# Two of batch 1's token tiles, instead of one, through all eight experts of layer 1

## The chip, the cores and the metric

The kernel runs on one core of a Trainium2 chip. The core has five engines with one instruction queue each, and each queue runs in order: TensorE (PE: matmuls and transposes, PEld its weight loads), VectorE (DVE), ScalarE (ACT), GpSimd (POOL) and SyncE (SP, which here only issues DMAs). The metric is the device time of one execution in microseconds (us). Before the change three runs gave 1483.84, 1483.90 and 1484.85 us; their median is 1483.9.

## The reference

The input x has 2 batches of 1024 tokens of 128 numbers, all in f32. Two layers follow, each an attention and a mixture of experts, with a layernorm ahead of each part and a residual sum behind it. The change lies in layer 1's mixture of experts:

```python
logits = relu(xf @ Wr1 + br1) @ Wr2 + br2
tg, ti = top_k(softmax(logits), 2)
tg = softmax(tg / 2)
out = silu(xf @ Ws1 + bs1) @ Ws2 + bs2            # shared expert, every token
for e in range(8):
    h = silu(xf @ We1[e] + be1[e]) @ We2[e] + be2[e]
    out = out + sum(tg * (ti == e)) * h           # two of eight experts a token
```

Each token needs two of the eight experts. The result is the same whether a token goes through its two experts alone, or through all eight with a weight of zero for six of them.

## The kernel before

A batch is 8 token tiles of 128. The instructions of PE, DVE, ACT and POOL stand in the order in which the Python code emits them (`manual_schedule`); those of SP are ordered by the framework's own planner. The parts of layer 1's experts are Python generators: each `next` emits one step, and the code around them decides whose step comes next.

- **Attention of layer 1** is a loop over `i` from 0 to 130. Unit `i` is (batch, query tile `qt`, head pair `pr`), with 8 units to a query tile, so batch 1 has the units 64 to 127 and iterations 128 to 130 drain the pipeline. One iteration issues the scores of unit `i` (L1082, PE), the maxima (L1090, DVE) and exponentials (L1112, ACT), the transposes of unit `i-1` (L1124, PE), their copies out of PSUM (L1130, ACT and DVE), and the product with the values of unit `i-2` (L1163, PE). The row of `qt` = 6 is batch 1's seventh, i = 112 to 119; that of `qt` = 7 is i = 120 to 127.
- **`route1(b, t0, nt)`** is the router of `nt` tiles, 9 steps (10 for one tile): statistics (L833), a root on POOL (L108), the normalised `y` on ACT (L840), transposes (L846) and an SP write of `y` to DRAM when `nt` > 1 (L849), a bias sum on POOL (L851), the two router matmuls (L856, L861), and the choice of two experts with some 20 small DVE operations and two of ACT (`picks`, L176 to L209).
- **`send1(b, nt)`** sorts the tokens of the first `nt` tiles by expert, one after another mostly on DVE: `places` (L280 to L321) and `tokens_of` (L335 to L375, with `2*nt` matmuls at L357). It takes 12 steps for 7 tiles, 11 for 6 (one 512-wide DVE step fewer). Sorted tokens are put into tiles of one expert each: `sorted_tiles(8)` = 23, `sorted_tiles(7)` = 21, `sorted_tiles(6)` = 19.
- **`experts1`** goes through the sorted tiles, one a step: a gather from DRAM on POOL (L911), a 256 KB weight load on SP (L898, four buffers `we1`), up-matmuls (L950), bias (L884, DVE), tanh (L887, ACT), L892 (DVE), down-matmuls (L958), a transpose of a later tile (L963), L966 (DVE), L941 (ACT) and a scatter to DRAM on POOL (L942). **`combine1`** reads the scattered rows back (L1017), adds them and stores the output (L1024, L1006).
- **`all_experts1(b, t)`** takes one tile in its own order through all eight experts, without sort, gather or scatter: L991, L884, L887, L892, L998, L1001, L984 and a sum on POOL (L985); 11 steps.
- **`shared1(b, n)`** is the shared expert of four tiles (L1044, L1055), 8 steps.

In the loop, `work(i)` emits one step of the list `side`, whose elements run one after another: `route1` and `send1` of batch 0, two `shared1`, `route1(1, 0, 4)`, and then, no earlier than i = `last` = 123, `route1(1, 4, 3)` and `send1(1, 7)`. It is called once an iteration from i = 67 on, and twice from `last` on. Every second iteration from 96 on emits one step of batch 0's `experts1`. What is left after the loop forms the tail:

- the rest of `side`, each step beside one of `route1(1, 7, 1)` and every second one beside a step of batch 0's experts;
- batch 0's remaining experts beside the first gathers of batch 1's (`after`), then `after` with 21 sorted tiles, beside both `shared1` of batch 1;
- tile 7 through `all_experts1`, beside `combine1` of tiles 0 to 6, and the last store.

Of the kernel before, what the change touches and what calls it, by code (L numbers as in the profile page):

```python
# [11 lines left out]
F32 = mybir.dt.float32  # L12
# [7 lines left out]
P = 128  # L20
# [3 lines left out]
NT = T // P  # L24
QB = 512
NQB = T // QB
TPB = QB // P
# [4 lines left out]
NE = 8  # L32
# [19 lines left out]
def two_layers(ctx, tc, a, out):  # L52
# [334 lines left out]
    with ExitStack() as st:  # L387
# [103 lines left out]
        N = len(units)  # L491
# [376 lines left out]
    def send1(b, nt):  # L868

        got = []  # L870
        yield from places(hots[b][:, :, :nt], got)
        rows, tiles_of[b] = got
        yield
        got = []
        yield from tokens_of(rows, gains[b][:, :, :nt], got)
        rows_of[b] = got
        yield
# [93 lines left out]

    def all_experts1(b, t):

        gate = small.tile([P, 2, NE], F32, tag="gate1", name="gate1", bufs=1)
        for k in range(2):
            nc.vector.tensor_tensor(gate[:, k, :], hots[b][:, k, t, :], bc(gains[b][:, k, t:t + 1], [P, NE]), ALU.mult)
        nc.vector.tensor_tensor(gate[:, 0, :], gate[:, 0, :], gate[:, 1, :], ALU.add)
        h, o = {}, {}
        up = {e: expert_weights(e) for e in range(UP_AHEAD)}
        for i in range(NE + 3):  # L980
            if i + UP_AHEAD < NE:
                up[i + UP_AHEAD] = expert_weights(i + UP_AHEAD)
            if i >= 3:
                nc.scalar.mul(o[i - 3], o[i - 3], gate[:, 0, i - 3:i - 2])  # L984
                nc.gpsimd.tensor_tensor(xs[b][:, t, :], xs[b][:, t, :], o.pop(i - 3), ALU.add)  # L985
            if 1 <= i <= NE:
                h[i - 1] = hidden1(*h[i - 1])
            if i < NE:
                ps = bank()
                for f in range(NI):  # L990
                    nc.tensor.matmul(ps[:, f * P:(f + 1) * P], up[i][:, f * P:(f + 1) * P], norms[b][:, t * P:(t + 1) * P],  # L991
                                     start=True, stop=True)
                h[i] = biased1(ps, be1[:, i * NI:(i + 1) * NI])
            if 2 <= i <= NE + 1:
                e = i - 2
                ps = bank()
                for f in range(NI):
                    nc.tensor.matmul(ps[:, :C], h[e][:, f * P:(f + 1) * P], we2[:, (e * NI + f) * C:(e * NI + f + 1) * C],  # L998
                                     start=(f == 0), stop=(f == NI - 1))
                o[e] = f1.tile([P, C], F32, tag="o1", name="o1", bufs=6)  # L1000
                nc.vector.scalar_tensor_tensor(o[e], ps[:, :C], 0.5, be2[:, e * C:(e + 1) * C], ALU.mult, ALU.add)  # L1001
            yield
# [5 lines left out]
    def combine1(b, nt, wait):  # L1008

        for _ in range(wait):  # L1010
            yield
        z = a1.tile([P, 2, NT, C], F32, tag="pT", name="z", bufs=2)
        groups = [(t0, min(TPB, nt - t0)) for t0 in range(0, nt, TPB)]
        for t0, n in groups:
            for k in range(2):
                rows = k * T + t0 * P
                nc.sync.dma_start(out=z[:, k, t0:t0 + n], in_=results[b][rows:rows + n * P, :].rearrange("(t p) c -> p t c", p=P))  # L1017
        for _ in range(4):
            yield
        for t0, n in groups:  # L1020
            yield
            xv = xs[b][:, t0:t0 + n, :]
            for k in range(2):
                nc.vector.tensor_tensor(xv, z[:, k, t0:t0 + n], xv, ALU.add)  # L1024
            store(b, t0, n)
# [34 lines left out]
    with ExitStack():  # L1060
        units = [(b, qt, pr) for b in range(NB) for qt in range(NT) for pr in range(8)]
        N = len(units)
# [121 lines left out]
        with tc.manual_schedule(engines={ET.PE, ET.DVE, ET.Activation, ET.Pool}):  # L1184
            steps = prepare(1)
            experts = experts1(0, NT, AHEAD)


            last = N // 2 + 8 * (NT - 1) + 3
            side = [(N // 2 + 3, route1(0, 0, TPB, "ckv", "lnT")), (0, route1(0, TPB, TPB, "ckv", "lnT")),  # L1190
                    (0, send1(0, NT)), (0, shared1(0, 0)), (0, shared1(0, 1)),
                    (N // 2 + 8 * TPB + 3, route1(1, 0, TPB, "k0", "k1")),
                    (last, route1(1, TPB, 3, "k0", "k1")), (0, send1(1, NT - 1))]

            def work(i):

                while side and i >= side[0][0] and next(side[0][1], N) is not None:
                    side.pop(0)

            issued = {}  # L1200

            def issue(i):
                s = scores(i)
                issued[i] = maxima(i, s)

            for i in range(N + 3):
                ends = units[i - 1][:2] if 1 <= i <= N and units[i - 1][2] == 7 else None
                ahead = short(i) and short(i + 1)
                if i < N and i not in issued:
                    if ahead:  # L1210
                        issue(i)
                    else:
                        s = scores(i)
                if ahead:

                    issue(i + 1)
                if 1 <= i <= N:
                    probsT[i - 1] = a1.tile([P, 2 * NT, P], F32, tag="pT", name="pT", bufs=2)
                    ps = fill(i - 1, 0)
                    if not short(i - 1):  # L1220
                        for r in range(2):
                            evict(i - 1, 0, r, ps, nc.scalar.copy)
                if i < N:
                    if i in issued:
                        exponentials(i, *issued.pop(i))
                    else:
                        exponentials(i, *maxima(i, s))
                if 1 <= i <= N and short(i - 1):
                    evict(i - 1, 0, 0, ps, nc.vector.tensor_copy)
                    evict(i - 1, 0, 1, ps, nc.scalar.copy)  # L1230
                if ends:
                    recips[ends] = reciprocals(ends)
                if i >= last:
                    work(i)
                if 2 <= i <= N + 1:
                    values(i - 2)
                    if units[i - 2] == (0, NT - 1, 7):
                        spread_values(1)
                if 1 <= i <= N and not short(i - 1):
                    ps = fill(i - 1, 1)  # L1240
                    for r in range(2):
                        evict(i - 1, 1, r, ps, nc.vector.tensor_copy)
                probs.pop(i - 1, None)
                if i >= 3 and units[i - 3][2] == 7:
                    project_out(*units[i - 3][:2])
                work(i)
                if i >= N // 2 + 8 * TPB and i % 2:
                    next(experts, None)
                if i < N:
                    b, qt, pr = units[i]  # L1250

                    if b == 0 and qt >= 2 and (i % 2 or qt >= NT - 2) and (left > 6 or (qt, pr) >= (NT - 2, 3)):
                        next(steps, None)
                        left -= 1
                    if (b, qt, pr) == (0, NT - 1, 4):
                        for _ in steps:
                            pass
                    if qt + 1 < NT and pr == 0:
                        mask_queries(b, qt + 1)
                    elif b + 1 < NB and (qt, pr) == (NT - 1, 5):  # L1260
                        mask_queries(b + 1, 0)

            def run(*steps):

                return any([next(g, N) is None for g in steps])


            half, rest = shared1(1, 0), chain(route1(1, NT - 1, 1, "k0", "k1"), shared1(1, 1))
            k = 0
            while side:  # L1270
                work(N)
                if k % 2 == 0:
                    run(experts)
                run(rest)
                k += 1
            after = experts1(1, NT - 1, 1)
            for k in range(AHEAD):
                run(after)
                run(half) if k % 2 else run(experts)
            while run(experts):  # L1280
                run(after)
            combining = combine1(0, NT, 6)
            while run(after):
                run(half) or run(rest)
                run(combining)
            while run(half) or run(rest):
                pass
            dense, combining = all_experts1(1, NT - 1), combine1(1, NT - 1, 0)
            while run(combining, dense):
                pass  # L1290
            store(1, NT - 1, 1)


# [67 lines left out]
```

## Time and profile before

| of the profiled execution | |
|---|---|
| its device time | 1485.42 us |
| its span, first to last instruction | 1483.6 us |
| mean granted TensorE clock | 0.977 |
| PE busy / PEld / DVE / ACT / POOL | 92% / 67% / 70% / 61% / 18% |
| chain that ended last, by engine | PE 70%, DVE 16%, ACT 6%, issue 5% |

The span is the time between the first and the last instruction in the trace. Busy is the time in which an engine ran at least one instruction. A row of the timeline gives start, duration, engine, line, operation, names and shape, the number of instructions merged into it, and in brackets the idle time of the engine before it and what ended it. A row of the windows view gives a stretch, its length, the busy time of PE, PEld, DVE, ACT and POOL with the instructions of each, the granted TensorE clock (1.00 is full), and the load of the DMA engines.

### The profile page before, as it was taken

Reading aid. Unit: us, or ns where it says so; the run is one execution under the profiler, and the core shown is the slowest. Engines: PE = TensorE matmul, PEld = TensorE weight load, DVE = VectorE, ACT = ScalarE, POOL = GpSimd, SP = SyncE. Lnnn points to the kernel's source line nnn. Section 1 sums busy time; section 2 is a strip of 40 time slices with the busy share of each in tenths; the row PEclk is TensorE's granted clock in tenths of the full one; section 3 lists DMA queues with packets and bytes.
Section 4 is the critical chain, followed back from the end, with each engine's and each line's share of the span. In section 5 each row is a group of like instructions: output and inputs, shape, how many; then the busy total and the mean of one; then the engine's idle time right before and its main releaser. Section 6 shows DMA issues by size and latency. Waiting matters only on the chain.

```text
span 1483.6 us, 40458 instructions
## 1 busy us (share of the span) xinstructions
PE 1369.4 (92%) x16931; PEld 986.8 (67%) x16931; DVE 1033.1 (70%) x2344; ACT 904.1 (61%) x1913; POOL 269.4 (18%) x246
## 2 busy tenths in 40 slices
PE   5999999999999999999998979999987899988787
PEld 3776777777777767777765555666754577757676
DVE  3776667777756867777457568677879467877476
ACT  4777567767755776776432257876665577753343
POOL 1010010000000100000154551012021212214553
PEclk9999999999999999999999989999989999999899
DMA  4000000000000000000110030000000011112443
GB/s 110 2 16 16 16 2 16 16 16 17 16 16 2 16 16 16 17 16 3 30 35 1 1 91 2 2 2 2 2 16 30 15 30 34 50 30 72 129 131 110
DMA packets 31318, 43.14 MB, mean 29 GB/s; under 512 B 7545, under 2 KB 19506, under 8 KB 31138
## 3 DMA queue, kind: packets, MB, share of 16 engines
q1 hardware_dynamic: 25216, 28.47, 6.9%
q0 software_dynamic: 4352, 10.70, 2.8%
q8 instruction: 134, 2.20, 0.6%
q10 hardware_dynamic: 1570, 1.41, 0.4%
q14 instruction: 46, 0.38, 0.1%
HBM read 35.51 MB, written 5.05 MB: 27 GB/s over the span
## 4 chain that ended last, share of the span: by engine, by line
PE 70%; DVE 16%; ACT 6%; issue 5%; another core or an unknown queue 1%; DMA 1%; POOL 0%; DVEq 0%; SPq 0%; ACTq 0%; POOLq 0%
PE ps_s L501 15%; PE ps_a L568 12%; PE ps_t L551 8%; PE ps_s L1082 8%; PE ps_t L1124 4%; PE ps_s L253 3%; PE ps_a L1163 3%; DVE ps_s L1090 3%; DVE p L510 3%; PE ps_a L486 2%; PE ps_t L950 2%; PE ps_t L958 2%; PE ps_t L583 2%; ACT p L1112 2%; DVE p L1090 2%
## 5 line engine op out<-in xcount | busy, mean ns | idle before, releaser
L510 DVE CUSTOM_DVE_ANT_0 p<-ps_s,zero 128x1024 f32<-128x1024 f32 x256 | 303.4, 1222 | 135.6 <-PE ps_s L501 134.3
L520 ACT ACTIVATE p<-p,nmx 128x1024 f32<-128x1024 f32 x256 | 293.1, 1153 | 3.1 <-DVE nmx L510 3.0
L557 ACT COPY pT<-ps_t 128x512 f32<-128x512 f32 x256 | 137.5, 589 | 197.7 <-PE ps_t L551 197.7
L501 PE MATMUL ps_s<-qk 64*128 64x512 f32 x1024 | 253.2, 609 | 1.9 <-DVE nmx L510 1.4
L568 PE MATMUL ps_a<-pT,zv 128*64 128x128 f32 x4096 | 251.8, 276 | 0.0
L568 PEld LDWEIGHTS ps_a<-pT,zv 128*64 128x64 f32 x4096 | 220.9, 137 | 9.3 <-issue 0.8
L551 PEld LDWEIGHTS ps_t<-ident,p 64*128 64x128 f32 x4096 | 159.9, 139 | 90.2 <-issue 86.5
L557 DVE COPY pT<-ps_t 128x512 f32<-128x512 f32 x256 | 164.6, 685 | 54.1 <-PE ps_t L551 54.1
L1082 PE MATMUL ps_s<-k,qm 64*128 64x512 f32 (+3 forms) x768 | 172.0, 536 | 16.6 <-ACT p L1112 11.7
L551 PE MATMUL ps_t<-ident,p 64*128 64x64 f32 x4096 | 177.5, 226 | 1.3 <-DVE pT L557 0.7
L1090 DVE CUSTOM_DVE_ANT_0 p<-ps_s,cmask 128x640 f32<-128x640 f32 (+3 forms) x128 | 126.0, 1022 | 71.8 <-PE ps_s L1082 60.7
L542 POOL TENSOR_TENSOR aoT<-aoT,recip 128x1024 f32<-128x1024 f32 x16 | 37.9, 2371 | 660.3 <-DMA recip<-flat 432.9
L501 PEld LDWEIGHTS ps_s<-qk 64*128 64x128 f32 x1024 | 92.9, 189 | 84.4 <-issue 74.5
L1124 PEld LDWEIGHTS ps_t<-ident,p 64*128 64x128 f32 x2304 | 106.4, 141 | 53.1 <-issue 25.5
L1130 ACT COPY pT<-ps_t 128x512 f32<-128x512 f32 (+3 forms) x192 | 95.8, 533 | 74.2 <-PE ps_t L1124 70.4
L1112 ACT ACTIVATE p<-p,nmx 128x640 f32<-128x640 f32 (+3 forms) x128 | 125.9, 992 | 4.6 <-DVE nmx L1090 4.5
L1082 PEld LDWEIGHTS ps_s<-k,qm 64*128 64x128 f32 x768 | 74.0, 196 | 82.1 <-issue 43.7
L1124 PE MATMUL ps_t<-ident,p 64*128 64x64 f32 x2304 | 119.3, 229 | 7.6 <-DVE pT L1130 2.9
L1163 PE MATMUL ps_a<-pT,vx 128*32 128x128 f32 x2304 | 99.1, 281 | 9.0 <-DVE pT L1130 8.3
L1130 DVE COPY pT<-ps_t 128x128 f32<-128x128 f32 (+3 forms) x192 | 87.2, 482 | 8.4 <-remote 5.9
L887 ACT ACTIVATE th<-h 128x512 f32<-128x512 f32 x52 | 32.8, 630 | 88.2 <-DVE h L884 78.4
L1112 ACT ACTIVATE p<-ps_s,nmx 128x128 f32<-128x128 f32 (+3 forms) x128 | 66.3, 525 | 31.3 <-DVE nmx L1090 30.6
(252 smaller groups left out, 1807.2 us busy)
## 6 DMA issues: line engine op xcount, KB each, us to landing
we<-in_we SPq DMA_DIRECT2D x52, 256.0 KB
recip<-flat SPq DMA_DIRECT2D x32, 256.0 KB
we<-in_we POOLq DMA_DIRECT2D x1, 2048.0 KB
z<-results SPq DMA_DIRECT2D x6, 256.0 KB
x<-in_x SPq DMA_DIRECT2D x4, 256.0 KB
up<-in_up_proj POOLq DMA_DIRECT2D x1, 1024.0 KB
normed<-y SPq DMA_DIRECT2D x3, 256.0 KB
out_x<-x SPq DMA_DIRECT2D x3, 256.0 KB
```

The costliest lines, as they stand in the source:

```text
L501: nc.tensor.matmul(s[h][:, n * QB:(n + 1) * QB], qk[rows, 0, qt * P:(qt + 1) * P], qk[rows, 1, n * QB:(n + 1) * QB], start=True, stop=True)
L510: nc.vector.tensor_tensor_reduce(p, s, bc(zero, [P, T]), -1.0, 3e38, ALU.add, ALU.min, nmx)
L520: nc.scalar.activation(p, p, AF.Exp, bias=nmx, scale=-1.0, accum_out=ssum[:, h, qt:qt + 1])
L551: nc.tensor.transpose(ps[r][:, k * 64:(k + 1) * 64], probs[i][h][rows, k * P:(k + 1) * P], ident[rows, rows])
L557: copy(probsT[i][h][:, :, r * 64:(r + 1) * 64], ps[r].rearrange("p (j q) -> p j q", q=64))
L568: nc.tensor.matmul(acc[h * D0:(h + 1) * D0, cols], zv[:, j, :], probsT[i][h][:, j, :], start=(j == 0), stop=(j == NT - 1))
L1082: nc.tensor.matmul(s[h][:, n * QB:n * QB + w], qms[b, qt][rows, pr, :], kTs[b][pr // 4][rows, n * QB:n * QB + w], start=True, stop=True)
L1090: nc.vector.tensor_tensor_reduce(to[:, :nk], s[:, :nk], cmask[:, T - nk:], -1.0, 3e38, ALU.add, ALU.min, nmx)
L1112: nc.scalar.activation(p[:, h, :nk], s[h][:, :nk], AF.Exp, bias=nmx[h], scale=-1.0, accum_out=sums[b, qt][:, head:head + 1])
L1124: nc.tensor.transpose(ps[r][:, c * 64:(c + 1) * 64], probs[i][rows, h, j * P:(j + 1) * P], ident[rows, rows])
L1130: copy(probsT[i][:, 8 * f:8 * f + n, r * 64:(r + 1) * 64], ps[r][:, :n * 64].rearrange("p (j q) -> p j q", q=64))
L1163: nc.tensor.matmul(acc[to * 32:(to + 1) * 32, k * P:(k + 1) * P], vx[:, j, g, pr % 4 * 24:pr % 4 * 24 + 32], probsT[i][:, h * (qt + 1) + j ...
```

## The change

The number of sorted tiles of batch 1 becomes `ND` = 6, and the tiles 6 and 7 go through `all_experts1`. `last` becomes 64 + 8*6 + 3 = 115, so the router of tiles 4 and 5 and the sort of six tiles may be emitted 8 iterations earlier, and `work` is called twice an iteration from 115 on. The router of tiles 6 and 7 (`prep`, 9 steps) stands after the loop, beside the first gathers and batch 0's experts. The second dense tile begins 8 steps after the first, and each has its own store. The small `gate1` tile gets a second buffer.

```diff
-        gate = small.tile([P, 2, NE], F32, tag="gate1", name="gate1", bufs=1)
+        gate = small.tile([P, 2, NE], F32, tag="gate1", name="gate1", bufs=2)
...
-            last = N // 2 + 8 * (NT - 1) + 3
+            ND = NT - 2
+            last = N // 2 + 8 * ND + 3
...
-                    (last, route1(1, TPB, 3, "k0", "k1")), (0, send1(1, NT - 1))]
+                    (last, route1(1, TPB, ND - TPB, "k0", "k1")), (0, send1(1, ND))]
...
-            half, rest = shared1(1, 0), chain(route1(1, NT - 1, 1, "k0", "k1"), shared1(1, 1))
-            k = 0
+            prep, half = route1(1, ND, NT - ND, "k0", "k1"), chain(shared1(1, 0), shared1(1, 1))
             while side:
                 work(N)
-                if k % 2 == 0:
-                    run(experts)
-                run(rest)
-                k += 1
-            after = experts1(1, NT - 1, 1)
+                run(experts)
+                run(prep)
+            after = experts1(1, ND, 1)
             for k in range(AHEAD):
                 run(after)
+                run(prep)
                 run(half) if k % 2 else run(experts)
+            while run(prep):
+                run(experts) or run(half)
             while run(experts):
                 run(after)
             combining = combine1(0, NT, 6)
             while run(after):
-                run(half) or run(rest)
+                run(half)
                 run(combining)
-            while run(half) or run(rest):
+            while run(half):
                 pass
-            dense, combining = all_experts1(1, NT - 1), combine1(1, NT - 1, 0)
-            while run(combining, dense):
+            def dense(t):
+                yield from all_experts1(1, t)
+                store(1, t, 1)
+            combining = chain(combine1(1, ND, 0))
+            first, second = dense(ND), dense(ND + 1)
+            for _ in range(NE):
+                run(combining, first)
+            while run(combining, first, second):
                 pass
-            store(1, NT - 1, 1)
```

## The prediction, made before the changed kernel ran

> **What bounds it now.** I read the page first, then the TensorE timeline of batch 1's last two attention rows, then the windows view of the stretch behind them, then the chain.
>
> ```profile
> span 1483.6 us, 40458 instructions
> PE 1369.4 (92%) x16931; PEld 986.8 (67%) x16931; DVE 1033.1 (70%) x2344; ACT 904.1 (61%) x1913; POOL 269.4 (18%) x246
> ```
>
> TensorE is the bound. The timeline shows how far this holds beside a side step. First the seventh row with one side step an iteration, then the eighth with two:
>
> ```profile
> 1255.20 1.77 PE L1082 MATMUL ps_s<-k,qm 64*128 64x512 f32 x8
> ...
> 1258.92 1.16 PE L950 MATMUL ps_t<-xT,we 128*128 128x128 f32 x8
> ...
> 1261.01 1.77 PE L1082 MATMUL ps_s<-k,qm 64*128 64x512 f32 x8
> ...
> 1264.73 0.66 PE L846 MATMUL ps_t<-ident,y 128*128 128x128 f32 x4
> 1265.32 1.77 PE L1082 MATMUL ps_s<-k,qm 64*128 64x512 f32 x8
> ...
> 1313.26 1.20 PE L846 MATMUL ps_t<-ident,y 128*128 128x128 f32 x3 [2.43 <-ACT y L840]
> 1314.39 3.53 PE L1082 MATMUL ps_s<-k,qm 64*128 64x512 f32 x8
> ...
> 1337.93 2.02 PE L958 MATMUL ps_t<-we,h 128*128 x8 [3.22 <-DVE pT L1130]
> ```
>
> With one step the matmuls follow without a gap: a unit costs 3.72 (1255.20 to 1258.92), an expert step 2.09 (to 1261.01), the router's transposes 0.59. With two, TensorE waits 2.43 for `y` and 3.22 for copies that stand on DVE behind `picks`, and the scores after the first gap take 3.53 instead of 1.77 to 1.99. The windows of the eighth row (two rows, drain included) and the tail:
>
> ```profile
> 1298.80:1328.50 29.70, 24.97 (x335) 16.97 (x334) 19.88 (x47) 16.64 (x35) 7.21 (x7) 0.94 0.16 37
> 1328.50:1349.30 20.80, 15.69 (x216) 12.38 (x212) 16.47 (x60) 8.23 (x19) 3.92 (x4) 0.92 0.14 31
> 1349.30:1364.70 15.40, 12.36 (x88) 11.26 (x88) 12.31 (x39) 5.29 (x16) 5.13 (x6) 0.89 0.24 77
> 1364.70:1389.50 24.80, 20.42 (x142) 19.04 (x142) 13.59 (x26) 10.38 (x25) 15.59 (x15) 0.86 0.42 113
> 1389.50:1457.00 67.50, 55.14 (x409) 48.94 (x408) 42.30 (x96) 29.21 (x72) 33.44 (x33) 0.95 0.49 135
> 1457.00:1483.60 26.60, 17.48 (x136) 15.85 (x136) 15.20 (x33) 8.40 (x18) 7.65 (x11) 0.96 0.34 102
> ```
>
> The tail is 134.3 us: A, the rest of the sort (15.4); B, sorted experts and shared expert (24.8 + 67.5 = 92.3); C, the dense tile (26.6). In B the chain holds two stops that no instruction explains:
>
> ```profile
> 1372.01 4.11 another core or an unknown queue
> ...
> 1392.97 6.79 another core or an unknown queue
> ```
>
> **Step count.** Sorted tiles go from 21 to 19, dense steps from 8 to 16: six expert steps more, all of them work for TensorE. They must be paid for by A and by waits.
>
> **C.** Steady dense steps:
>
> ```profile
> 1463.93 1.16 PE L998 MATMUL ps_t<-we,h 128*128 128x128 f32 x8 [0.54 <-DVE h L884]
> 1464.93 1.06 PE L991 MATMUL ps_t<-lnT,we 128*128 128x128 f32 x8
> 1465.98 1.16 PE L998 MATMUL ps_t<-we,h 128*128 128x128 f32 x8
> ```
>
> They repeat every 2.05 us. The second tile starts 8 steps after the first and overlaps its last three, so C gains 8 x 2.05 = +16.5. Its eight weight loads are on SP three to four steps (6 to 8 us) ahead; the first tile's store stands between them on SP and waits for its last sum on POOL, about one step, which that lead covers; uncovered it would cost 2. The read-back of results (L1017, issued 1462.36 in the profile) stays at the start of C. The second `gate1` buffer only lets the second tile's three small DVE operations go ahead: 0.
>
> **B.** Before, B holds 9 - 3 = 6 steps of batch 0 and 21 of batch 1. The two shared experts take about 14.2 there (for each four L1044 groups of 0.86 and two L1055 groups of 1.8). So an expert step costs (92.3 - 14.2) / 27 = 2.89, stops and half clock included. After: A's three steps join, 9 + 19 = 28 steps, 80.9, plus 14.2. The router for two tiles brings nine steps where B had four. Its root on POOL now queues behind gathers and scatters (0.98 + 0.30 each), and DVE, in order, waits for it with the experts' bias sums behind; it also writes 128 KB of `y` on SP that nobody reads, ahead of weight loads with three steps' lead. I take 3 for the five extra steps (0 if the experts cover them, 6 if each delays a step by a DMA issue). B becomes 98.1. A and B together go from 107.7 to 98.1, -9.6; the tail by -9.6 + 16.5 = +6.9.
>
> **Attention.** `side` needs 75 steps after; 48 are called before i = 115, the rest at two an iteration, so it ends at i = 128: no sort is left for the tail and A goes. The price is 14 iterations at double rate (115 to 128) where there were 8 (123 to 130), of which 13 instead of 5 lie in full attention. The five cost: i = 123 to 126 took 29.7 us; their own TensorE work is 4 x 4.05 (eighth-row unit, 1298.79 to 1302.84) + 2 x 2.09 + 1.9 for the router = 22.3; i = 127 took 11.6 (1328.46 to 1340.10) against 6.15. Together 12.9 us of loss, 2.6 an iteration. The single-rate row above lost nothing. For after I take: i = 115 to 118, `route1(1, 0, 4)` with `y` and its transposes in one iteration as in the row of 2.43: 4 x 2.6 = 10; i = 118 to 122, the router of two tiles, with `y` and transposes in different iterations: half, 6; the sort, i = 123 to 128: DVE needs 4.5 an iteration for attention and experts plus 9.7 / 5.5 for the sort (11.0 us for seven tiles), 6.3 against some 5.5 on TensorE: 7. Sum 23, so +10. Between what ends lie these? Below, 0 (all like the single-rate row); above, 13 x 2.6 = 34. Further, L357 and the sort's other matmuls move into full rows, +2.5; the drain loses DVE's sort operations ahead of the last output (1345.07 to 1348.18), -3. Attention: +9.5.
>
> **Two rules weighed.** After the 2.43 gap and inside the 3.22 one the granted clock fell to half: 1.5 lost in the scores and 1.4 at 1337.93 and behind. The Trainium skill (TensorE: Matmul & The Clock Gate, "Why this matters for your kernels") asks for no idle gap over about 3 us between matmuls. Read so, most of the new gaps (1 to 2.6 us) would keep the clock, and the 23 fall to about 18: 5 us less. I keep the row. Against my forecast speaks the skill's Perfetto Trace Analysis, "Optimization Strategy": regimes with different bounds may gain by interleaving. By it A's work other than its experts vanishes beside attention, attention costs 0, and the sum is +7. The row without gaps says that attention has no free TensorE time, only that a single step costs nothing beyond its own work.
>
> **Sum.** +9.5 + 6.9 = +16.4, rounded down to +15 because the sort's and router's costs are taken from the worst iterations. The profiled span, 1483.6, is 0.3 below the median of the runs, 1483.9; the profiled device time, 1485.4, is 1.5 above. I add to the median: **1499 us**; likeliest case alone 1492 to 1507.
>
> **Rivals.**
> - *Attention hides it* (the interleaving rule): double rate costs nothing more than before. 1483.9 + 6.9 = 1491. For it: the seventh row, where the router now runs, has a little less DVE work (maxima of 1.0 to 1.1 us instead of 1.1 to 1.2). Against: the waits for `y` are of order, not of load.
> - *Faster, by the loss of the last five iterations going away.* If the 12.9 belongs to the eighth row's full DVE and not to the double rate, it vanishes with the router moved up. Then attention is -12.9 + 2.5 - 3 plus what the new 14 iterations lose. At nothing lost: 1483.9 - 13.4 + 6.9 = 1477. It decides where they lose under 3.6 us together. Against: the sort still sits in the eighth row, with more DVE work than the router's.
> - *The stops go away.* The stops of 4.1 and 6.8 fall where POOL issues gathers back to back, and half clock follows (6.8 us lost in B). With gathers spread over other steps they may not come: -17.7 on the sum, about 1482, no change. Nothing names their cause, so I can't say that they go.
> - *Worse:* all 13 iterations lose 2.6: +11 more, 1510; the same if the dense pair waits for weights.
> - *It doesn't do what it says:* a sort still open at the loop's end. The count excludes it.
>
> **Chances.** Main case 0.48, hidden in attention 0.17, faster 0.15, stops gone 0.08 (a quarter of it below 0.2%, the rest within), worse 0.12. Measurement tells 0.2%, 3 us, from no change. Faster 0.17, same 0.06, slower 0.77. The range leaves out most of the faster case and the end of the worse one: 1481 to 1510.
>
> **What would show it.** Right: 16 L991 groups instead of 8 at about 2.05, C near 43 us; no L357 behind the last L1163; gaps over 1 us ahead of L846 or L958 from i = 115 on; last scores some 10 us later than 1328.46. Wrong: last scores not later than before; expert steps in B under 2.5 us; a gap ahead of L991 released by a DMA.

## The result and the profile after

The changed kernel takes **1505.4 us** in the median of four runs (1502.98 to 1510.41), the kernel before 1484.4 in four runs beside it: a ratio of **1.0134 [1.0113, 1.0155]**, slower by 21 us. The forecast was 1499, with a range of 1481 to 1510. The execution that was profiled took 1502.98 us, the lowest of the four, and that of before 1485.42, 1.0 above its median, so the traces show 17.5 us of the difference (span 1501.1 against 1483.6) and not the whole 21.

The first lines of the page of after: the span, then busy time, share and instructions of each engine.

```profile
span 1501.1 us, 40680 instructions
PE 1382.3 (92%) x17021; PEld 997.3 (66%) x17021; DVE 1042.3 (69%) x2363; ACT 910.3 (61%) x1923; POOL 270.4 (18%) x250
```

TensorE is busy 12.9 us longer than before, part of it at half clock; the other 4.6 us of the longer span are waits.

I cut both traces at four marks that exist in both: the scores of unit 114, the scores of unit 123, the last projection of the attention (L1179), and the first matmul of a dense tile (L991). The windows view of before:

```profile
1250.36:1298.79 48.43, 48.00 (x684) 35.58 (x683) 42.01 (x106) 35.21 (x76) 11.54 (x11) 1.00 0.15 47
1298.79:1349.19 50.40, 40.56 (x544) 29.24 (x544) 36.26 (x106) 24.88 (x53) 11.13 (x11) 0.93 0.16 34
1349.19:1457.99 108.80, 88.99 (x642) 80.34 (x643) 68.40 (x160) 45.27 (x114) 54.88 (x54) 0.92 0.44 121
1457.99:1483.60 25.61, 16.52 (x130) 14.86 (x128) 15.12 (x32) 8.00 (x17) 6.93 (x10) 0.96 0.36 106
```

and of after:

```profile
1253.10:1315.82 62.72, 54.07 (x692) 39.28 (x691) 46.55 (x131) 36.69 (x80) 13.30 (x14) 0.95 0.14 39
1315.82:1361.65 45.83, 39.88 (x559) 30.27 (x559) 36.25 (x94) 23.65 (x50) 7.83 (x8) 0.96 0.14 31
1361.65:1458.72 97.07, 79.89 (x584) 71.24 (x583) 60.97 (x138) 43.25 (x107) 52.74 (x50) 0.95 0.45 129
1458.72:1501.10 42.38, 32.66 (x258) 29.68 (x256) 27.24 (x59) 15.38 (x33) 11.57 (x18) 0.95 0.37 111
```

| stage | before | after | difference | forecast |
|---|---|---|---|---|
| units 114 to 123 | 48.4 | 62.7 | +14.3 | |
| unit 123 to last projection | 50.4 | 45.8 | -4.6 | attention in all +9.5 |
| sorted tail (A and B) | 108.8 | 97.1 | -11.7 | -9.6 |
| dense tail (C) | 25.6 | 42.4 | +16.8 | +16.5 |

The last 2.7 us lie ahead of unit 114; 2.0 of them in the first 42 us of the kernel, where the change touches nothing. The first line of each fence is the finding: in the seventh row TensorE went from 48.00 busy of 48.43 at full clock to 54.07 of 62.72 at 0.95. It has only 8 matmuls more there: of the 14.3 us, 8.2 are waits and 6.1 are busy time, most of it matmuls at a lower clock.

The TensorE timeline of after shows the waits that were named:

```profile
1263.79 1.56 PE L846 MATMUL ps_t<-ident,y 128*128 128x128 f32 x4 [2.07 <-ACT y L840]
1265.14 1.94 PE L950 MATMUL ps_t<-xT,we 128*128 128x128 f32 x8
...
1281.33 1.16 PE L958 MATMUL ps_t<-we,h 128*128 x8 [1.34 <-DVE pT L1130]
...
1301.31 0.62 PE L856 MATMUL ps_t<-lnT,wr 128*32 128x256 f32 x2 [2.28 <-ACT lnT L847]
1301.86 3.08 PE L1082 MATMUL ps_s<-k,qm 64*128 64x512 f32 x8
...
1343.25 2.15 PE L1082 MATMUL ps_s<-k,qm 64*128 64x512 f32 x7
```

`y` of the first four tiles comes 2.07 late, and its transposes then take 1.56 where they took 0.66 before; the expert step (L950), which doesn't use `y`, stands behind them in the queue and waits too; the router matmul of tiles 4 and 5 waits 2.28 for the transposed tile, and the scores behind it take 3.08. The last scores stand at 1343.25, 14.8 later than at 1328.46.

The dense tail, TensorE and then SP's queue:

```profile
1484.80 1.16 PE L998 MATMUL ps_t<-we,h 128*128 128x128 f32 x8
1485.80 1.06 PE L991 MATMUL ps_t<-lnT,we 128*128 128x128 f32 x8
1486.85 1.16 PE L998 MATMUL ps_t<-we,h 128*128 128x128 f32 x8
```

```profile
1482.43 0.34 SPq L1006 DMA_DIRECT2D out_x<-x  x1
1482.88 0.37 SPq L898 DMA_DIRECT2D we<-in_we  x1
```

The dense steps repeat every 2.05 us as before. The first tile's store does stand between the weight loads on SP, and no L991 group waits for a DMA behind it.

### The profile page after: what moved, and what is told of

It reads as the page before. It is cut to its first block, busy times and chain, and to the rows that moved or that the text cites. A ratio compares the mean times of both kernels' runs of the same rounds, so it can differ in the third digit from the quotient of the medians.

```text
span 1501.1 us, 40680 instructions
## 1 busy us (share of the span) xinstructions
PE 1382.3 (92%) x17021; PEld 997.3 (66%) x17021; DVE 1042.3 (69%) x2363; ACT 910.3 (61%) x1923; POOL 270.4 (18%) x250
## 4 chain that ended last, share of the span: by engine, by line
PE 69%; DVE 17%; ACT 6%; issue 5%; another core or an unknown queue 1%; DMA 1%; POOL 0%; ACTq 0%; SPq 0%; DVEq 0%; POOLq 0%
PE ps_s L501 15%; PE ps_a L568 12%; PE ps_t L551 8%; PE ps_s L1082 7%; PE ps_t L1124 3%; PE ps_s L253 3%; PE ps_a L1163 3%; DVE ps_s L1090 3%; DVE p L510 2%; PE ps_a L486 2%; PE ps_t L958 2%; PE ps_t L583 2%; PE ps_t L950 2%; ACT p L1112 2%; PE ps_t L718 1%
## 5 line engine op out<-in xcount | busy, mean ns | idle before, releaser
L1082 PE MATMUL ps_s<-k,qm 64*128 64x512 f32 (+3 forms) x768 | 172.8, 538 | 16.7 <-ACT p L1112 11.8
L1163 PE MATMUL ps_a<-pT,vx 128*32 128x128 f32 x2304 | 99.0, 280 | 9.1 <-DVE pT L1130 8.5
L887 ACT ACTIVATE th<-h 128x512 f32<-128x512 f32 x58 | 36.6, 630 | 91.3 <-DVE h L884 72.4
```

Of the source, the lines that this page charges most:

```text
L1082: nc.tensor.matmul(s[h][:, n * QB:n * QB + w], qms[b, qt][rows, pr, :], kTs[b][pr // 4][rows, n * QB:n * QB + w], start=True, stop=True)
L1163: nc.tensor.matmul(acc[to * 32:(to + 1) * 32, k * P:(k + 1) * P], vx[:, j, g, pr % 4 * 24:pr % 4 * 24 + 32], probsT[i][:, h * (qt + 1) + j ...
```

## The experiments

The kernels ran on several chips, and these differ: the kernel before takes 1484 us on the first one, 1459, 1456 and 1486 on three others. So each run is read by its ratio to the kernel before on its own chip, and by its stages. Some expectations give absolute times made for the first chip; on a faster chip these don't apply and their ratios do. All stages in one table (us):

| kernel | 114 to 123 | 123 to projection | sorted tail | dense tail | ratio to before |
|---|---|---|---|---|---|
| before, first chip | 48.4 | 50.4 | 108.8 | 25.6 | |
| after, first chip | 62.7 | 45.8 | 97.1 | 42.4 | 1.0134 [1.0113, 1.0155] |
| before_again | 48.4 | 48.1 | 88.6 | 25.7 | one execution |
| after_again | 61.8 | 46.3 | 83.2 | 42.4 | 1.0098 [1.0060, 1.0137] |
| e1_double123 | 48.4 | 42.7 | 91.4 | 42.1 | 1.0048 [1.0030, 1.0067] |
| e2_single | 48.4 | 37.7 | 98.0 | 42.0 | 1.0093 [1.0071, 1.0116] |
| e3_one_dense | 61.8 | 44.8 | 81.5 | 25.0 | 1.0007 [0.9989, 1.0025] |
| e4_plain_gather | 61.6 | 44.8 | 79.4 | 44.2 | 1.0113 [1.0092, 1.0133] |
| s7_shared_late | 46.0 | 49.4 | 104.1 | 25.6 | 1.0025 [1.0011, 1.0038] |
| s6_shared_late | 47.2 | 46.1 | 95.6 | 42.1 | 1.0086 [1.0059, 1.0112] |
| e5_parity | 58.9 | 52.1 | 97.1 | 42.1 | 1.0110 [1.0090, 1.0130] |
| e6_prep_spread | 62.7 | 45.7 | 94.2 | 42.4 | 1.0098 [1.0074, 1.0121] |
| b1_double127 | 48.5 | 39.6 | 114.0 | 25.6 | 0.9966 [0.9955, 0.9976] |

e1 to e4 ran on the chip of 1459, the two repeats, s7 and s6 on that of 1456, e5, e6 and b1 on that of 1486.

### Two steps an iteration only from i = 123, as before

Six sorted and two dense tiles stay, and so do the units at which router and sort may start; only the second step an iteration comes later. The router of tiles 6 and 7 moves behind what is left of the sort.

```diff
-                if i >= last:
+                if i >= N // 2 + 8 * (NT - 1) + 3:
                     work(i)
...
             while side:
                 work(N)
                 run(experts)
-                run(prep)
```

> Edit: the changed kernel, but two side steps an iteration only from i = 123 on; the router of tiles 4 and 5 may still start at 115. The end of the sort (3 or 4 steps) falls behind the loop, beside batch 0's experts. Theory (the double rate costs): iterations 114 to 122 fall from 62.7 us to about 48 as before the change, 123 to the last projection rises from 45.8 to about 50, sorted tail 97 to about 101: -6, 1497 to 1501 us. Rival (a side step costs the same at any rate, only the six added expert steps cost): attention stays near 108 us, the tail grows by the left sort, 1507 to 1511.

Units 114 to 123 went back to 48.4, from 61.8 in e3, which has after's attention and ran on the same chip. The stretch behind, now with sort steps at double rate, took 42.7, less than expected. The tail pays for the sort steps left over: 91.4 against 81.5. The windows view of e1, first three stages:

```profile
1245.82:1294.23 48.41, 47.99 (x684) 35.60 (x683) 42.00 (x106) 35.11 (x76) 11.52 (x11) 1.00 0.15 47
1294.23:1336.89 42.66, 37.47 (x541) 27.80 (x541) 35.94 (x106) 24.17 (x52) 10.76 (x11) 0.96 0.17 38
1336.89:1428.30 91.41, 81.75 (x609) 72.66 (x608) 64.09 (x151) 43.52 (x109) 51.98 (x50) 0.96 0.45 137
```

The same router of tiles 0 to 3 runs beside the same attention units here, TensorE is busy 47.99 of 48.41, and the clock is full. So neither the router nor the seventh row costs the 13 us, but the second step in an iteration. From unit 114 to the projection it is 91.1 against 106.7 in e3, 15.6 less, and the tail gives 9.9 of that back. The ratio is 1.0048, against 1.0098 in after_again on another chip; the two intervals still overlap, so the reading rests on the stages of one chip.

### One step an iteration to the end

```diff
-                if i >= last:
-                    work(i)
...
-                run(prep)
```

> Edit: the changed kernel with one side step an iteration throughout; the whole sort of six tiles stands behind the loop, each step beside a step of batch 0's experts. Theory (the double rate costs): from unit 114 to the last projection 84 to 88 us instead of 108.5, no idle gap of TensorE over 1 us ahead of a router matmul; sorted tail up from 97 to about 112; total 1492 to 1503. Rival (steps cost the same at any rate): 11 fewer steps of about 1 us there, attention 97 to 100, and a total of 1508 or more.

Attention has no loss left: from unit 114 to the last projection 86.1 us (48.4 and 37.7). TensorE's timeline of e2 at the places where after waits for `y` and for the transposed tile:

```profile
1259.66 0.66 PE L846 MATMUL ps_t<-ident,y 128*128 128x128 f32 x4
...
1263.96 1.05 PE L856 MATMUL ps_t<-lnT,wr 128*32 128x512 f32 x2
...
1308.61 0.44 PE L846 MATMUL ps_t<-ident,y 128*128 128x128 f32 x2
...
1316.24 0.62 PE L856 MATMUL ps_t<-lnT,wr 128*32 128x256 f32 x2
```

There is no bracket of idle time in these lines. But the sort, which is mostly a serial chain on DVE, now runs ahead of the last gathers with nothing but experts beside it: the tail takes 98.0 against 81.5 in e3, +16.5. At 1.0093 the kernel is not shown to be better than after. The double rate costs in attention and saves in the tail, and by nearly the same amount (against e3, 20.5 less in attention and 16.5 more in the tail).

### One dense tile only

Tile 7's routed experts are left out; its store stays.

```diff
-            first, second = dense(ND), dense(ND + 1)
+            first, second = dense(ND), iter([])
...
+            store(1, ND + 1, 1)
```

> Edit: the changed kernel without the second dense tile: tile 7 is stored without its routed experts (8 expert steps left out). Theory: the dense part falls from 42.4 us to about 25.6 and nothing else moves: 16 to 17 us less, 1487 to 1490. Rival (the second tile mostly fills waits of the first, or moves loads of the sorted part): 10 us less or fewer, 1495 or more.

The dense tail shrinks from 42.0 or 42.1 (e1, e2, same chip) to 25.0, and the ratio to 1.0007. Eight more dense steps cost 17 us, and they hide behind nothing: the whole price of the second tile reaches the end.

### Gathers by plain loads

The gathered tokens are replaced by tiles in their own order, loaded by SP, so that POOL issues no gathers; the expert tiles work on the wrong tokens.

```diff
-                nc.gpsimd.indirect_dma_start(out=got[s], ...)
+                nc.sync.dma_start(out=got[s], in_=normed[b][s % nt * P:(s % nt + 1) * P, :])
```

> Edit: the changed kernel with every gather of the sorted experts replaced by a plain SP load of 128 rows in their order, so the experts get the wrong tokens, with the same amount of work; the scatters stay on POOL. Theory A (gathers issued back to back on POOL cause the unexplained stops of about 4 us): no stop in the sorted tail, expert step there 2.3 to 2.5 us instead of 2.85, total 10 to 18 us less, 1488 to 1496. Theory B (the stops have another cause): they stay, tail within 4 us of 97, total 1501 to 1509.

This settles nothing about the stops of 4 to 7 us. On this chip e3, with the gathers in place, has none either, so there was nothing to remove. The sorted tail, 79.4 against 81.5, shows only that the gathers themselves cost little; the dense tail, 44.2 against 42.0 and 42.1 in e2 and e1, takes the 2 us back.

### Both kernels again on one chip

No edit: after in four executions and before in one more, to have both traces from a chip without the stops.

> No edit: the changed kernel once more, beside the next three. On the chip of the first four experiments the time before was 1459 us, the unexplained stops were gone, and the sorted tail of the kernel without its second dense tile took 81.5 us. Theory (the loss is attention and the dense tile, which hardly depend on the stops): ratio 1.012 to 1.015 wherever it runs. Rival (the stops make part of the loss): a ratio nearer to 1.008 on a chip without stops.

> No edit: the kernel before, for its trace on the same chip as the others of this call. Without stops: tail from the last projection 118 to 124 us instead of 134.4; attention from unit 114 to the last projection within 2 us of 98.8.

The ratio, 1.0098, lies between the theory's and the rival's, and its interval takes in both. The runs of after spread from 1471.3 to 1477.6, and the profile is of the highest. Before's tail from the last projection on takes 114.3 here, below the 118 to 124 expected, and its attention 96.5, 2.3 under the 98.8. The windows view of before on this chip, the last three stages:

```profile
1290.97:1339.05 48.08, 38.71 (x545) 28.58 (x544) 36.26 (x106) 24.87 (x53) 11.13 (x11) 0.96 0.16 36
1339.05:1427.60 88.55, 82.05 (x642) 75.03 (x643) 67.73 (x160) 44.72 (x114) 57.47 (x54) 0.98 0.50 148
1427.60:1453.30 25.70, 16.56 (x130) 14.91 (x129) 15.12 (x32) 8.00 (x17) 6.94 (x10) 0.96 0.35 105
```

and of after:

```profile
1303.80:1350.14 46.34, 40.88 (x559) 30.83 (x559) 36.37 (x94) 23.75 (x50) 7.83 (x8) 0.93 0.14 30
1350.14:1433.30 83.16, 77.23 (x584) 69.30 (x583) 60.71 (x138) 43.00 (x107) 52.19 (x50) 0.96 0.50 150
1433.30:1475.70 42.40, 32.67 (x258) 29.70 (x256) 27.26 (x59) 15.37 (x33) 11.57 (x18) 0.98 0.37 111
```

Seen by stages (after less before): +13.3, -1.7, **-5.4**, +16.7, and -0.5 ahead of unit 114; together the 22.4 by which the spans differ. The sorted tail saves half of what it saved on the first chip. The tail of before holds no stop here and is 20 us shorter; the fewer steps of after are then worth less.

### The shared experts of batch 0 moved out of the attention

If the early double rate is dear because router and sort come too late for single steps, room can be made: batch 0's two shared experts leave `side` and run in the tail instead. Once with seven sorted tiles (s7, built on before), once with six (s6, built on after with double rate from 123). In the tail, `half` is emitted once an iteration beside the gathers and batch 0's experts, and twice in the first five (s7) or three (s6) iterations of the last loop over `after`.

```diff
-                    (0, send1(0, NT)), (0, shared1(0, 0)), (0, shared1(0, 1)),
+                    (0, send1(0, NT)),
...
-            half, rest = shared1(1, 0), ...
+            half, rest = chain(shared1(0, 0), shared1(0, 1), shared1(1, 0)), ...
```

> Edit on the kernel before (one dense tile, last = 123): both shared experts of batch 0 leave the attention rows and run in the tail, beside the gathers and the sorted experts. Theory (TensorE has no free time in the rows, but waits in the tail): iterations 99 to 113 lose the 14 us of the shared experts, the tail grows by 4 to 14: ratio 0.990 to 1.000. Rival (the tail's waits are stops that no work fills): the tail grows by the full 14 or more, ratio 1.000 to 1.004.

> Edit on the changed kernel: as e1 (double rate only from 123), and batch 0's shared experts in the tail, so that the routers run one step an iteration and the sort alone runs at two. Theory: attention from unit 114 to the last projection 88 to 91 us and 14 us less in iterations 99 to 113, tail 4 to 14 more than e1's: ratio 0.998 to 1.005. Rival (e1's ratio came from the sort left behind the loop, not from the rate): 1.005 to 1.012.

s7 is slower than before by 0.25%, and its tail grows by 15.5, as the rival had it: the move loses. s6 is slower than before by 0.86%, in its rival's range, and can't be told from after (1.0098 on the same chip). In s7 unit 114 starts 8.9 us earlier than in before_again (1233.63 against 1242.54) and the last projection 10.0 (1329.04 against 1339.05), less than the 14.2 that the shared experts take in the tail. The windows view of s7's sorted tail:

```profile
1329.04:1433.10 104.06, 97.96 (x722) 86.46 (x723) 75.30 (x172) 54.94 (x130) 55.72 (x55) 0.97 0.44 127
```

TensorE is busy 97.96 where before_again had 82.05, +15.9, and the 6.5 us in which it stood still there are 6.1 here: the moved work fills none of this tail's waits and is paid in full. The rows had covered about 4 us of it.

s6 also shows the sort at two steps an iteration with the routers at one: from unit 123 to the projection it takes 46.1, at full clock, against 37.7 in e2 with single router steps in the same stretch. From unit 114 on s6 takes 93.4, over the 88 to 91 expected: the sort alone also costs when it runs at two steps.

### The double rate one iteration later

This changes which router steps fall into one iteration: the step of `y` and that of its transposes are separated for tiles 0 to 3 and joined for tiles 4 and 5.

```diff
-                if i >= last:
+                if i >= last + 1:
                     work(i)
```

> Edit: the changed kernel with two side steps an iteration from i = 116 instead of 115, so every router step pairs with the other neighbour. Theory (the waits are of order: some pair that hands over between engines within one iteration always costs): the idle gap ahead of the transposes of tiles 0 to 3 (2.07 us in the changed kernel) goes, one of over 1 us appears elsewhere, ahead of L856 or of the transposes of tiles 4 and 5; iterations 115 to 122 stay within 3 us of the changed kernel's 56.9. Rival (one bad pair makes most of the loss): they fall by 6 us or more.

The TensorE timeline of e5:

```profile
1265.03 0.66 PE L846 MATMUL ps_t<-ident,y 128*128 128x128 f32 x4 [0.45 <-ACT xT L970]
...
1268.52 1.04 PE L856 MATMUL ps_t<-lnT,wr 128*32 128x512 f32 x2 [1.32 <-ACT lnT L847]
...
1294.75 0.86 PE L846 MATMUL ps_t<-ident,y 128*128 128x128 f32 x2 [2.81 <-ACT y L840]
...
1319.38 1.01 PE L958 MATMUL ps_t<-we,h 128*128 x3 [2.77 <-DVE pT L1130]
```

The gap of 2.07 for `y` is gone; a gap of 2.81 for `y` has come two tiles later, 1.32 for the transposed tile, and 2.77 among the sort steps. Units 115 to 123 take 54.1 against 57.9 in after, 3.8 less where the theory allowed 3 and the rival asked for 6, but 123 to 127 take 32.2 against 27.4; from 115 to 127 it is 86.3 against 85.3 (86.0 in after_again). So which step shares an iteration decides where the wait falls, and this shift left the sum as it was.

### The router of tiles 6 and 7 spread over more steps

Its nine steps are emitted every second time, beside the gathers and the experts that follow.

```diff
             for k in range(AHEAD):
                 run(after)
-                run(prep)
+                if k % 2 == 0:
+                    run(prep)
...
-            while run(prep):
-                run(experts) or run(half)
+            for k in range(2):
+                run(experts)
+                run(half)
```

The loops behind it call `run(prep)` every second time too.

> Edit: the changed kernel with the router of tiles 6 and 7 emitted one step every second iteration of the tail, instead of nine steps in a row beside the gathers; two shared-expert steps stand in the freed place. Theory (that router costs 8 us and not 3 where its chain crosses POOL, DVE and ACT every step): sorted tail 77 to 81 us instead of 83.2, total 2 to 6 us under the changed kernel's. Rival (its cost is its own work): tail within 1.5 us of 83.2.

The sorted tail takes 94.2 against 97.1 in e5 on the same chip. Each of the two holds one unexplained stop, 6.09 in e6 and 4.09 in e5; without them it is 88.1 against 93.0. That points to a cost of some 5 us for the dense router steps in after, but one profile each, with stops of changing length, doesn't show it. The ratio, 1.0098, overlaps that of e5.

### The kernel before with the double rate at the last unit only

If the second step costs in full attention, before pays for it as well, from i = 123 on. Here it starts at i = 127.

```diff
-                if i >= last:
+                if i >= N - 1:
                     work(i)
```

> Edit on the kernel before: two side steps an iteration only from i = 127 instead of 123. Theory (double rate costs a router about 1 us a step in full rows, while a step behind the loop costs 1.2 to 1.5): unit 114 to the last projection 90 to 92 us instead of 96.5, the rest of the sort behind the loop 4 steps longer, +5: ratio 0.997 to 1.002. Rival (the eighth row's loss is the row's own): attention 95 or more, ratio 1.003 to 1.006.

The ratio over 20 runs is 0.9966 [0.9955, 0.9976], 1481.2 against 1486.3 us: **faster than before**, just beyond the range expected, and after was slower than before on both chips where it ran. The windows view of b1, the second and third stage:

```profile
1304.31:1343.87 39.56, 36.85 (x545) 28.09 (x544) 33.42 (x87) 24.82 (x54) 9.89 (x10) 1.00 0.17 39
1343.87:1457.90 114.03, 92.42 (x643) 82.23 (x644) 71.20 (x179) 45.44 (x114) 55.85 (x56) 0.90 0.40 116
```

The eighth row has the full clock and takes 39.6 us where before took 50.4 in its first profile and 48.1 on the chip of 1456: the attention gains 10.8 or 8.5. What the tail gives back is not settled. It takes 114.0 against 108.8 in the first profile, 5.2 more, but that tail of before holds 10.9 us of stops and b1's holds none; on the chip of 1456, without stops, before's took 88.6. (The two spans, 1483.5 and 1483.6, don't show the gain, since b1 comes 5.5 us later to unit 114, where the kernels are still the same.) So the gain of 5.0 us is shown by the medians on one chip; how much of it hangs on the stops, and whether b1 would win on a chip without them, is open.

## Why the prediction was right, and where it was off

- **Slower, by the dense tile and the double rate:** right. Undone alone, the dense tile takes the ratio to 1.0007 (e3, with one tile's experts missing), the early double rate to 1.0048 (e1). After itself did not run on the chip of e1 and e3; its ratio was 1.0134 and 1.0098 on two others. The median lies in the likeliest case's own range, 1492 to 1507, near its upper end.
- **C, +16.5:** measured +16.8 and +16.7. The store on SP and the second `gate1` buffer cost nothing, as said.
- **Attention, +9.5:** measured +9.7 on the first chip (14.3 - 4.6) and +11.6 on the chip of 1456 (13.3 - 1.7). The single losses there, each against the same units in e2 with one step an iteration: i = 115 to 118 took 29.3 against 21.2, 8.1 lost (forecast 10); i = 119 to 122 took 27.7 against 22.4, 5.2 (forecast 6); i = 123 to 126 took 29.1 against 23.1, 6.0 (forecast 7, up to 128). On the first chip they are 7.2, 7.1 and 4.4. So they sum to 19, not 23; and from unit 127 to the last projection the first chip's trace shortened by 2.3 (20.7 to 18.4), where the forecast's terms make about 6 (5.5 and 3 less, some 2 of the sort's 7 more). Two errors of about 4 cancel: the mechanism was right, the closeness of the total is in part luck. One reason was wrong: tiles 4 and 5 were to lose half because `y` and its transposes fall into different iterations. Their L846 indeed has no gap, but L856 then waits 2.28 for the transposed tile. e5 shows that the other pairing doesn't help.
- **A and B, -9.6:** measured -11.7 on the first chip. The stops inside are 10.9 before (4.11 and 6.79) and 8.4 after, here in the chain of after:

```profile
1391.60 4.17 another core or an unknown queue
...
1412.98 4.21 another core or an unknown queue
```

  Without them it is -9.2. On the chip without stops it is -5.4. **This is the term that was mis-sized.** The 2.89 for an expert step held the stops; without them the tail of before_again gives (88.6 - 15.4 - 14.2) / 27 = 2.19, if A took the 15.4 of the first profile. Twenty-eight such steps and the shared experts make 75.5, and the 83.2 measured leave 7.7 for the router of tiles 6 and 7, where I took 3. That the router costs 7.7 is argued from this sum; e6 points the same way and doesn't settle it.
- **The sum** was +16.4 and was rounded down to +15 because the costs were taken from the worst iterations. They were not too high: spans differ by 17.5 and 22.4, medians by 21.1 and 17.3. Rounding down was a mistake. Of the 21.1 on the first chip, 3.6 are not in the trace, since the profile of after is of its fastest run (2.5) and that of before of one above its median (1.0); where the slower runs of after lose theirs stays open.
- **Rivals.** *Attention hides it* fell: units 114 to 123 lengthened by 14.3, with the waits of order that were held against it. Its sum of +7 is close to what e1 measured (0.48%, 7 us of 1459), but only in number, since e1 still leaves sort steps to the tail. What holds of the interleaving rule here is that one step an iteration cost nothing beyond its own work. *The last five iterations' loss goes away* was half true: that stage does get shorter, by 4.6 and 1.7 instead of 12.9, and the new iterations lose far more than the 3.6 at which it would have decided. b1 collects this loss in the attention without paying for new ones there; what its tail pays is open. *The stops go away* fell: they stayed on the first chip, and on a chip without any, after is still slower by 0.98%. *Worse* fell: the 12 iterations lost 19 us and not 2.6 each, and no weight load was late.
- **The clock rule.** It was weighed against the row of 2.43. After's gaps of 2.07 and 2.28, both shorter than the 3 us that the Trainium skill gives (TensorE: Matmul & The Clock Gate, "Why this matters for your kernels"), were followed by matmuls at about half speed: 1.56 for 0.66, and 3.08 for 1.99. So was e1's gap of 1.72, by scores of 3.06. Keeping the row was right. But the length of a gap doesn't settle it: on the chip of 1456 the same wait of 2.43 in before was followed by scores at full speed,

```profile
1305.01 1.09 PE L846 MATMUL ps_t<-ident,y 128*128 128x128 f32 x3 [2.43 <-ACT y L840]
1306.04 1.99 PE L1082 MATMUL ps_s<-k,qm 64*128 64x512 f32 x8
```

  and so was the wait ahead of L856 in after_again, 2.14 long (scores of 1.99). That stage of before ran at a clock of 0.96 there and took 48.1, against 0.93 and 50.4 on the first chip.
- **What was to be seen:** the last scores are 14.8 later where some 10 were said, and the sort ends inside the attention, as TensorE's timeline of after has it:

```profile
1347.90 2.81 PE L357 MATMUL ps_t<-place_hot,hot 128*38 128x128 f32 x24
...
1358.20 1.08 PE L1163 MATMUL ps_a<-pT,vx 128*32 128x128 f32 x30 [1.50 <-DVE pT L1130]
```

  The last L357 stands ahead of the last L1163, so A is gone. An expert step in B takes (97.1 - 14.2) / 28 = 2.96 on the first chip, over the 2.5 below which I would have been wrong, but 2.46 on the chip without stops: another sign that 2.89 was a price with stops in it.

## What to carry to other kernels

A dependent side chain that was woven into a full in-order engine cost only its own work at one step per unit of the main work, and waits at the hand-overs at two; moving the same steps by one unit only moved the waits. Before work is pulled forward, compare what its late place costs in the tail with what the denser weave costs, since the right place may be later and not earlier: here four iterations later were worth 5.0 us on the one chip where that was timed. Going without the sort for one more tile costs eight expert steps for two saved ones: on the chip without stops the dense tail grew by 16.7, and the sorted one, though the rest of the sort had left it, shrank by only 5.4.

## What the runs showed of the hardware that was not expected

- The stops of 4 to 7 us, at which the chain names no instruction, come on the chips where before takes 1484 to 1486 us and not on those where it takes 1456 or 1459. The stretch from unit 98 to 99 takes 11.18 us with one and 4.56 without. In their course DVE stands and TensorE soon runs dry, while POOL goes on issuing gathers and scatters, as in before's longest:

```profile
1396.19 0.99 POOL L942 DMA_INDIRECT results<-o,s_to  x1 [0.30 <-issue]
1397.48 0.98 POOL L911 DMA_INDIRECT back<-normed,s_id  x1 [0.30 <-issue]
1399.79 0.69 DVE L1057 SCALAR_TENSOR_TENSOR x<-ps_t,x 128x512 f32<-128x512 f32 x1 [6.82 <-remote]
...
1400.54 2.08 PE L1044 MATMUL ps_t<-lnT,ws 128*128 128x512 f32 x2 [5.17 <-DVE x L1057]
```

  POOL issues them back to back in before_again too, and DVE doesn't stop there. The cause stays open: the kernel that replaced the gathers ran on a chip without stops.
- Where TensorE has neither a wait nor a stop, the attention agrees from chip to chip to 0.04 us: units 114 to 123 of before take 48.43 on the first chip and on that of 1456, and the same units in e1 and b1 48.41 and 48.45 on the two others. The two spans of before differ by 30.3 us all the same; 16.8 of them are its three stops, and 20.3 fall into the sorted tail, with two of these.
- Runs of one kernel on one chip spread by up to 10 us (before on the chip of 1459: 1453.4 to 1463.5), so that 5 us, b1's gain, needs many runs to be seen.
